# A conditioned transformer block on one core: two more products of the ff residual taken by a second level of seven products, seven big tiles in place of eight

## The chip, the cores and the metric

The kernel runs on one NeuronCore of one Trainium2 chip. The metric is the device time of one execution in microseconds (us), the median of several runs; a profile of one execution stands beside it. The engines are called as the profile calls them: PE is the matrix engine (PEld its weight loads), DVE the vector engine, ACT the scalar engine, POOL the GpSimd engine, SP the engine whose queue issues most DMAs. [...]

## The reference

The input x is 2 x 2048 rows of 512 floats, with a condition t of 512 floats for each half. All is float32.

```python
emb = silu(t) @ ada_w + ada_b
shift_msa, scale_msa, gate_msa, shift_mlp, scale_mlp, gate_mlp = split(emb, 6)
norm  = ln(x) * (1 + scale_msa) + shift_msa
h     = gelu_exact(norm @ ssm_w1 + ssm_b1)            # 512 -> 512
x     = x + gate_msa * (h @ ssm_w2 + ssm_b2)          # 512 -> 512: the ssm residual
norm2 = ln(x) * (1 + scale_mlp) + shift_mlp
hf    = gelu_tanh(norm2 @ ff_w1 + ff_b1)              # 512 -> 1024
x     = x + gate_mlp * (hf @ ff_w2 + ff_b2)           # 1024 -> 512: the ff residual
```

## The kernel before

**Tiles and blocks.** The 4096 rows are cut into eight blocks of 512 rows (128 partitions x 4 chunks). A block's x, its normalised and transposed form nT, hA (the ssm's hidden layer) and hClo and hChi (the two halves of the ff's hidden layer) are "big" tiles of 1 MB each, from a pool of eight. A tile asked for when all are in use takes over one whose last user comes earlier in program order, and waits for that user.

**Seven products for eight.** A matrix product is split into 2 x 2 quarters and computed from seven products P1 to P7 of quarters and of sums of quarters. The sums (`sums_of_first` for one operand, `sums_of_second` for the other) are made by POOL or DVE. A product accumulates in one of three PSUM banks, called y (P1, P6, P7, P4), x (P2) and v (P5, P3), and DVE adds the bank to the residual tile after each product, so that what a bank holds is always the sum that the next quarter of the result needs. In the residuals the banks are seeded with the bias row, by ACT.

**The ff residual.** For blocks 1 to 7 this is `residual_in_leaves`. P1, P5, P6 and P7 are "plain": eight fp32 matmuls with 256 columns (16 records in the trace, L724), read by DVE at L735. P2, P3 and P4 go by a second level: each is split into seven again. These are the leaves: two fp32 matmuls with 128 columns each (four records, L757). The loop over the leaves has seven turns, one for each of LEAVES = P1, P2, P6, P5, P7, P3, P4; in a turn PE does that leaf of P2 and of P3, which lie side by side in one bank and are read by one 256-wide add (L773), then that leaf of P4, in a bank of its own, read by a 128-wide add (L776). Two matmuls of plain P7 are put into each of the first four turns, and P7 is read in turn 4. Block 0 uses seven plain products (`residual`, L465 and L687).

**The order of the work.** It is written out by hand: each engine gets its instructions in program order, and work that is not the current stage's is hung on "hooks", places between products of the current stage. From block 1 on, one pass of the main loop (i = 1 to 7) does in PE's order:

1. the ff products of block i (`Second.products`, L881): 26 products by a longer scheme; its operand "forms" are 20 sums made from nT of the second norm (L819, on POOL, in the pass before), and its results are added by ACT (L895) and DVE (L898) and put through gelu by ACT (L876);
2. the ssm residual of block i+1 (oA, L465 and L687), which ends with the second norm's statistics of block i+1 (L499, L500);
3. the ff residual of block i (oC);
4. the ssm hidden layer of block i+2 (hA, L465).

In the last two passes some of these stages have no block left. A norm is: statistics on DVE, `scales` on POOL (L508 to L526), `normal` on ACT (L539), `turn` on DVE (a transpose inside 32 x 32 blocks, L550), `move` (16 DMAs of 64 KB, L559, on SP's queue or shared with ACT's), and `moved` on ACT (scale and shift, L582). The first norm of block i+2 is made during stage 1 of pass i, the second norm of block i+1 during stage 3.

In stage 3, the first product's hook holds the load of x of block i+3, the scales and normalisation of the second norm and the sums of nT of block i+2; after P5, after P6 and in the turns come the transposes, the move and the statistics of block i+3. The sums for the leaves of P2 and P4 ("sums24", four adds of 128 x 512) and of P3 ("sums3", four of 128 x 256) are made by POOL in stage 2. From block 4 on the gates of the second half of the batch apply: w2 and fw2 are loaded again and multiplied by the new gate on DVE (L395), which is set off in blocks 2 and 3.

Of the kernel before, what the change touches and what calls it, by code (L numbers as in the profile page):

```python
# [140 lines left out]
def kernel(  # L141
# [16 lines left out]
    nc = tc.nc  # L158
# [13 lines left out]
    big = ctx.enter_context(tc.tile_pool(name="big", bufs=8))  # L172
# [58 lines left out]
    brows = big_tile("brows")  # L231
# [176 lines left out]
    fw2_t = const.tile([P, 3, 3, KD // 2, P], F32, tag="fw2_t", name="fw2_t")  # L408
# [3 lines left out]
    single_t = fw2_t[:, 2]  # L412

    def leaves_of_weight(w_sb, s, eng):


        def views(w):
            v = w.rearrange("p (h k) (q e d) -> p h k q e d", h=2, e=2, d=P)
            return {f"{h + 1}{e + 1}": v[:, h, :, :, e, :] for h in range(2) for e in range(2)}

        hi = w_sb[:, w_sb.shape[1] // 2 :, :]
        q23, q4 = views(hi), {n: v[:, :, 0, :] for n, v in views(s[:, 2]).items()}
        t23, t4 = thirds(pair_t), thirds(single_t)
        o23, o4 = second_operands(q23, t23), second_operands(q4, t4)
        ops = {
            "P2": {n: v[:, :, 0, :] for n, v in o23.items()},
            "P3": {n: v[:, :, 1, :] for n, v in o23.items()},
            "P4": o4,
        }
        return ops, sums_of_second(q23, t23, eng) + sums_of_second(q4, t4, eng)  # L430
# [7 lines left out]
    def seed(name, row, part):  # L438


        b, cols = (("y", row[:, : D // 2]), ("v", row[:, D // 2 :]))[part]
        t = ps_g.tile([P, 2, HT], F32, tag=b, name=f"p{b}_{name}_{len(seeds.get((name, b), ()))}")
        seeds.setdefault((name, b), []).append(t)
        nc.scalar.copy(t, cols.unsqueeze(1).to_broadcast([P, 2, HT]))
# [41 lines left out]
    class Norm:  # L486
# [44 lines left out]
        def normal(self, c, eng=None, on_pe=False):  # L531

            if c == 0:
                self.nT = big_tile(f"nT{self.name}")
                self.xn = self.blocks().rearrange("p m k c q -> p m (k c q)") if on_pe else self.nT
# [172 lines left out]
    def residual_in_leaves(name, i, hops, wops, leaf_wops, kdim, hooks, last=False, read_p7=4):  # L708
# [3 lines left out]
        F = D // 2  # L712
        q = {
# [26 lines left out]
        for p, dests, n in (("P1", ("11",), "P1"), ("P5", ("22", "12"), "P2"), ("P6", ("12",), "P6")):  # L740
            run(plain(p))
            read(p, *dests)
            hooked(n)

        tags = {("P23", "y"): "t", ("P23", "x"): "x", ("P23", "v"): "x", ("P4", "y"): "t", ("P4", "x"): "y", ("P4", "v"): "v"}
        leaf_ps = {
# [3 lines left out]
        started = set()  # L750

        def leaf(which, n, f):
            t = leaf_ps[which, LEAF_BANK[f]]
            fresh = (which, LEAF_BANK[f]) not in started
            started.add((which, LEAF_BANK[f]))
            for k in range(KD // 2):
                nc.tensor.matmul(  # L757
                    t[:, n, :],
                    hops.leaves["P4" if which == "P4" else ("P2", "P3")[n]][f][:, k, :],
                    leaf_wops["P4" if which == "P4" else ("P2", "P3")[n]][f][:, k, :],  # L760
                    start=((fresh or f == "P2") and n == 0 and k == 0),
                    stop=(f in ("P2", "P3", "P4") and k == KD // 2 - 1),
                    skip_group_check=True,
                )

        p7 = list(plain("P7"))
        places = {1: "P5", 2: "R2", 3: "P7", 4: "R4", 5: "P3", 6: "P4"}
        for r, f in enumerate(LEAVES):
            t, e = LEAF_AT[f]
            for n in range(2):  # L770
                leaf("P23", n, f)
            d = xt[:, t, :].rearrange("p (q d) -> p q d", q=2)[:, :, e * P : (e + 1) * P]
            nc.vector.tensor_tensor(d, leaf_ps["P23", LEAF_BANK[f]][:, :2, :], d, ALU.add)  # L773
            leaf("P4", 0, f)
            d = xt[:, 2 + t, e * P : (e + 1) * P]
            nc.vector.tensor_tensor(d, leaf_ps["P4", LEAF_BANK[f]][:, 0, :], d, ALU.add)  # L776
            if r == read_p7:
                read("P7", "22", "21")
# [10 lines left out]
            now, p7 = p7[: PLAIN_P7[r]], p7[PLAIN_P7[r] :]  # L789
            run(now)  # L790
            if r in places:
                hooked(places[r])
# [48 lines left out]
    class Second:  # L841


        def __init__(self, i):
            self.i, self.lo, self.hi = i, big_tile(f"hClo_{i}"), big_tile(f"hChi_{i}")
            self.parts = {}
# [61 lines left out]
        def summed(self, g, eng, cut=1):  # L908
            s = thirds(sums.tile([P, 3, 2, HT], F32, tag="s", name=f"hSC_{self.i}_{g}"))
# [8 lines left out]
        def leaf_sums(self, room24, room3, eng):  # L918


            v = self.hi.rearrange("p (g k) (q e t) -> p g k q e t", g=2, q=2, e=2)
            q24 = {f"{e + 1}{g + 1}": v[:, g, :, :, e, :] for e in range(2) for g in range(2)}
            q3 = {
                f"{e + 1}{g + 1}": self.parts[g]["P3"][:, :, e * P : (e + 1) * P]
                for e in range(2)
                for g in range(2)
            }
            s24 = thirds(room24.rearrange("p (s k q t) -> p s k q t", s=3, k=2, q=2))
            s3 = thirds(room3.rearrange("p (s k t) -> p s k t", s=3, k=2))
            o24, o3 = first_operands(q24, s24), first_operands(q3, s3)  # L930
# [3 lines left out]
                "P3": o3,  # L934
            }
            return sums_of_first(q24, s24, eng), sums_of_first(q3, s3, eng)

        def leaf_room(self, nxt, nx2):
            L = 3 * KD // 2 * P
            if nxt and not nx2:  # L940
                return [big_tile(f"leaves_{self.i}_{n}").rearrange("p a b -> p (a b)")[:, : m * L] for n, m in ((0, 2), (1, 1))]
            flat = forms.rearrange("p n a r -> p (n a r)")
            return flat[:, : 2 * L], flat[:, 2 * L : 3 * L]
# [212 lines left out]
    fold, late_forms = None, []  # L1156


    for i in range(1, NBLK):
        nxt, nx2, last = i + 1 < NBLK, i + 2 < NBLK, i + 1 == NBLK  # L1160
# [4 lines left out]
        if i == 1:  # L1165
            leaf_wops, ops = leaves_of_weight(fw2_sb, fw2_s, nc.gpsimd)
            hook(hooks, (5, 7, 9, 11, 13, 14, 15, 16), ops)
        if i == 1:
            hook(hooks, (0,), [n1[i + 2].scales])
        if nxt:  # L1170
            hook(hooks, (1, 2, 3, 4), hA[i + 1].summed(nc.gpsimd))
        if nxt:
            hook(hooks, (20, 24), [lambda p=p: seed(f"oA_{i + 1}", gb[2], p) for p in range(2)])
        else:
            hook(hooks, (20, 24), [lambda p=p: seed(f"oC_{i}", gb[5], p) for p in range(2)])
        if nx2:
            hook(hooks, (12, 14, 16, 18), [lambda c=c: n1[i + 2].normal(c) for c in range(C)])
            hook(hooks, (14, 16, 18, 20), [lambda c=c: n1[i + 2].turn(c) for c in range(C)])
            hook(hooks, (20,), [n1[i + 2].move])
        if fold:  # L1180
            hook(hooks, (0,), fold[:2])
            hook(hooks, (5,), fold[2:6])
        hook(hooks, (0, 0, 0, 1), late_forms)
# [6 lines left out]
        late_forms = []  # L1190
# [3 lines left out]
        sums24, sums3 = hC.leaf_sums(*hC.leaf_room(nxt, nx2), nc.gpsimd)  # L1194
        hook(hooks, ("P5",), sums24)
        hook(hooks, ("P7",), sums3)
        if nxt:
# [3 lines left out]
            if fold:  # L1201
                hook(hooks, ("P1", "P2", "P6", "P5"), fold[6:10])
            hook(hooks, ("P2", "P6"), [lambda p=p: seed(f"oC_{i}", gb[5], p) for p in range(2)])
# [6 lines left out]
        leaf_fold, fold = fold and fold[10:], None  # L1210

        hooks = {}
        if i + 3 < NBLK:
            n1[i + 3] = Norm(i + 3, 1)
            hook(hooks, ("P1",), [lambda: load_x(i + 3)])
        if nxt:

            hook(hooks, ("P1",), [lambda: n2[i + 1].scales(on_dve=not nx2)])
            hook(hooks, ("P1",), [lambda c=c: n2[i + 1].normal(c) for c in range(C)])
# [5 lines left out]
        if i + 3 < NBLK:  # L1225
            hook(hooks, ("P5", "P7", "P3", "P4"), n1[i + 3].stats())
            hook(hooks, ("P4",), [n1[i + 3].scales])
# [10 lines left out]
        if not last:  # L1238
            hook(hooks, ("P4",), [lambda: store(i, 0)])
        refold5 = (i + 1) % PER_B == 0 and nxt  # L1240
        if refold5:
            b = (i + 1) // PER_B
            gb[5], multiply_5 = gate_bias(5, b, fb2, f"gb5_{b}")
            hook(hooks, ("P7",), [lambda: load_half("fw2", fw2, fw2_sb, 0)])
        if nxt:
# [7 lines left out]
            if not nx2:  # L1253

                def late_form(n):
                    if n == 0:
                        late["ops"] = form((nc.vector,) * 12 + (nc.gpsimd,) * 8)
                    late["ops"][n]()

                late_forms = [lambda n=n: late_form(n) for n in range(len(HK_B))]  # L1260
                hook(hooks, ("P7",) * 4 + ("R4",) * 4, late_forms[:8])
                late_forms = late_forms[8:]

        residual_in_leaves(f"oC_{i}", i, hC, fw2_ops, leaf_wops, KH // 2, hooks, last, 4 if nx2 or last else 6)
        if refold5:
            load_half("fw2", fw2, fw2_sb, 1)
        if not last:
# [4 lines left out]
        if refold5:  # L1272
            take_gate(5, b)
            fw2_ops, fold = weight_of_second(fw2_sb, fw2_s, gate[5, b], (nc.vector,))
            leaf_wops, ops = leaves_of_weight(fw2_sb, fw2_s, nc.vector)
            fold += ops
        hooks = {}
        if refold5:
            hook(hooks, ("P6",), [multiply_5])
            hook(hooks, ("P5", "P5", "P7", "P3", "P4", "P4"), fold[:6])  # L1280
            fold = fold[6:]
        if refold2:
            take_gate(2, b)
            w2_ops, w2_fold = weight_of_second(w2_sb, w2_s, gate[2, b], (nc.vector,))
            hook(hooks, ALL, [multiply_2] + w2_fold)
        if nx2:
            hA[i + 2] = First(i + 2, n1[i + 2].ops, hooks)
# [45 lines left out]
```

## Time and profile before

| | us |
|---|---|
| median of 3 runs | 594.19 (592.70 to 594.46) |
| profiled execution | 592.64 |
| its span, first to last instruction | 590.8 |
| outside the span | 1.8 |

| engine | busy us | share of the span |
|---|---|---|
| PE | 581.2 | 98% |
| PEld | 512.9 | 87% |
| DVE | 402.6 | 68% |
| POOL | 396.1 | 67% |
| ACT | 236.0 | 40% |

The granted clock of PE is 1.000 over the span. Busy time of PE is the union of records whose ends are modelled: a record overlaps the next one, so that PE can be 98% busy and its instructions still start at an even pace. The pace is read from the starts.

### The profile page before, as it was taken

What the parts mean: (1) busy time and instruction counts of PE and PEld (TensorE: products, weight loads), DVE (VectorE), ACT (ScalarE), POOL (GpSimd) and SP (SyncE); (2) the same over time, 40 slices, a digit from 0 to 9 for tenths busy, and PEclk for the clock granted to TensorE, in tenths of its full rate; (3) what the DMA queues carried; (4) which work ended last, traced back from release to release, by engine and by line L of the source; (5) the groups of instructions that cost most, each with busy time, mean ns of one, the idle gap of its engine ahead of it and who ended that gap; (6) DMA issues with size and microseconds to landing.
All of it is one profiled execution on the core that took longest, in us unless ns stands there. A gap on an engine that the chain in (4) does not pass through costs nothing.

```text
span 590.8 us, 8982 instructions
## 1 busy us (share of the span) xinstructions
PE 581.2 (98%) x3127; PEld 512.9 (87%) x3127; DVE 402.6 (68%) x723; ACT 236.0 (40%) x400; POOL 396.1 (67%) x480
## 2 busy tenths in 40 slices
PE   7999999999999999999999999999999999998997
PEld 4888888888889888998889988898888988897886
DVE  4978888897567475675755778874756446569663
ACT  2235457305532364234721456124553236222420
POOL 1875359999980968539984599948687294804260
PEclk9999999999999999999999999999999999999999
DMA  8990333300324104440152702231030400031002
GB/s 317 395 388 11 86 72 79 101 37 36 72 73 116 46 0 103 155 136 2 24 137 60 226 1 50 94 72 72 1 72 1 143 2 1 1 72 71 1 1 72
DMA packets 24376, 50.17 MB, mean 85 GB/s; under 512 B 4576, under 2 KB 5644, under 8 KB 23436
## 3 DMA queue, kind: packets, MB, share of 16 engines
q1 hardware_dynamic: 20608, 44.86, 24.5%
q10 hardware_dynamic: 3724, 4.75, 3.3%
q8 instruction: 25, 0.41, 0.3%
q14 instruction: 19, 0.16, 0.1%
HBM read 26.51 MB, written 8.40 MB: 59 GB/s over the span
## 4 chain that ended last, share of the span: by engine, by line
PE 95%; DVE 2%; DMA 2%; SPq 0%; issue 0%
PE py_oC L724 12%; PE px_hC L881 10%; PE py_hA L465 9%; PE py_oA L465 9%; PE py_hC L881 8%; PE pv_hC L881 8%; PE pl_oC_P_y L757 6%; PE pv_hA L465 5%; PE pv_oA L465 5%; PE pv_oC L724 4%; PE pl_oC_P_v L757 3%; PE px_hA L465 2%; PE py_oC L465 2%; PE py_hC L465 2%; PE px_oA L465 2%; DMA ada<-in_L_cond_ada_w_dram 2%
## 5 line engine op out<-in xcount | busy, mean ns | idle before, releaser
L582 ACT ACTIVATE nT<-nT,mod,mod 128x512 f32<-128x512 f32 x54 | 39.6, 803 | 103.0 <-DMA nT<-blocks 54.1
L539 ACT ACTIVATE nT<-x,nmr,rstd 128x512 f32<-128x512 f32 x56 | 42.5, 804 | 52.9 <-POOL nmr L526 38.0
L724 PE MATMUL py_oC<-fw,hClo 128*128 128x256 f32 x224 | 54.1, 379 | 0.0
L508 POOL TENSOR_SCALAR ve<-mv 128x4 f32<-128x4 f32 x16 | 3.7, 232 | 72.4 <-DVE mv L500 65.7
L499 DVE BATCH_NORM_STATS2 st<-x 128x6 f32<-128x512 f32 x64 | 43.4, 678 | 5.2 <-DMA x<-in_x_dram 4.9
L347 POOL TENSOR_TENSOR hSC<-hClo,hChi 128x512 f32<-128x512 f32 (+1 forms) x17 | 20.5, 1213 | 37.9 <-ACT hChi L876 24.4
L724 PEld LDWEIGHTS py_oC<-fw,hClo 128*128 128x128 f32 x224 | 40.4, 190 | 4.3
L881 PE MATMUL py_hC<-forms,fw 128*128 128x256 f32 x168 | 40.8, 379 | 0.0
L898 DVE TENSOR_TENSOR hClo<-hClo,py_hC 128x512 f32<-128x512 f32 x42 | 28.5, 681 | 17.3 <-ACT hClo L895 9.6
L819 POOL TENSOR_TENSOR forms<-forms 128x256 f32<-128x256 f32 x51 | 38.1, 748 | 3.0
L550 DVE STREAM_TRANSPOSE blocks<-nT 128x512 f32<-128x512 f32 x56 | 38.0, 695 | 1.6 <-ACT nT L539 1.2
L819 POOL TENSOR_TENSOR forms<-nT,forms 128x256 f32<-128x256 f32 x38 | 27.7, 749 | 15.9 <-DVE forms L819 15.4
L881 PEld LDWEIGHTS py_hC<-forms,fw 128*128 128x128 f32 x168 | 31.8, 190 | 4.4
L687 DVE TENSOR_TENSOR x<-py_oA,x 128x512 f32<-128x512 f32 x32 | 22.0, 688 | 19.4 <-PE py_oA L465 14.3
L898 DVE TENSOR_TENSOR hChi<-hChi,pv_hC 128x512 f32<-128x512 f32 x35 | 23.3, 683 | 14.3 <-PE pv_hC L881 14.3
L465 PE MATMUL py_hA<-nT,w 128*128 128x256 f32 x128 | 30.4, 380 | 0.0
L881 PE MATMUL px_hC<-forms,fw 128*128 128x256 f32 x112 | 27.8, 380 | 2.1 <-DVE forms L819 2.1
L876 ACT ACTIVATE hClo<-hClo,colsT 128x256 f32<-128x256 f32 x56 | 25.3, 500 | 4.9 <-DVE hClo L898 4.4
L895 ACT ACTIVATE hClo<-px_hC 128x512 f32<-128x512 f32 x21 | 12.5, 597 | 35.0 <-PE px_hC L881 30.1
L465 PE MATMUL py_oA<-w,hA 128*128 128x256 f32 x112 | 26.5, 379 | 0.0
L465 PEld LDWEIGHTS py_hA<-nT,w 128*128 128x128 f32 x128 | 23.7, 190 | 3.1 <-DVE hA L639 0.2
L876 ACT ACTIVATE hChi<-hChi,colsT 128x256 f32<-128x256 f32 x56 | 25.1, 496 | 1.9 <-DVE hChi L898 1.9
(291 smaller groups left out, 1584.0 us busy)
## 6 DMA issues: line engine op xcount, KB each, us to landing
nT<-blocks SPq DMA_DIRECT2D x168, 64.0 KB
x<-in_x_dram SPq DMA_DIRECT2D x7, 1024.0 KB
out_dram<-x SPq DMA_DIRECT2D x14, 512.0 KB
ada<-in_L_cond_ada_w_dram SPq DMA_DIRECT2D x6, 1024.0 KB
fw<-in_L_cond_ff_w_dram SPq DMA_DIRECT2D x2, 2048.0 KB
nT<-blocks ACTq DMA_DIRECT2D x56, 64.0 KB
w<-in_L_cond_ssm_w_dram SPq DMA_DIRECT2D x3, 1024.0 KB
fw<-in_L_cond_ff_w_dram SPq DMA_DIRECT2D x2, 1024.0 KB
```

The source lines that it names most:

```text
L465: nc.tensor.matmul(ps[b][j * apart][:, j, :], lhs(p, j, k), rhs(p, j, k), start=(fresh and j * (not apart) == 0 and k == 0), stop=(p in (" ...
L499: nc.vector.bn_stats(st, xs[self.i][:, c, :])
L539: nc.scalar.activation(t, x_c, AF.Identity, bias=self.nmr[:, c : c + 1], scale=self.rstd[:, c : c + 1])
L550: nc.vector.transpose(self.bl[:, :, :, c, :].rearrange("p m k q -> p k m q"), self.nT[:, c, :].rearrange("p (k m q) -> p k m q", k=KD, m=C),)
L582: nc.scalar.activation(dst, src, AF.Identity, bias=shift, scale=scale)
L687: nc.vector.tensor_tensor(d, ps[BANK[p]][:, js], d, ALU.add)
L724: yield lambda j=j, k=k: nc.tensor.matmul(ps[BANK[p]][:, j, :], hops(p, j, k), wops[p][:, k, :], start=False, stop=(k == kdim - 1), skip_g ...
L757: nc.tensor.matmul(t[:, n, :], hops.leaves["P4" if which == "P4" else ("P2", "P3")[n]][f][:, k, :], leaf_wops["P4" if which == "P4" else ( ...
L819: eng.tensor_tensor(reg[d], reg[a], reg[b], ALU.add if f == "+" else ALU.subtract)
L876: nc.scalar.activation(h, h, AF.Gelu_apprx_tanh, bias=fb1T[:, m : m + 1])
L881: nc.tensor.matmul(ps[b][:, j, :], fa[ra][:, j * P : (j + 1) * P], fb[rb].rearrange("p a (c q) -> p c a q", q=Q), start=(fresh and j == 0) ...
L898: nc.vector.tensor_tensor(dest(d), dest(d), ps[b], op)
```

## The change

In blocks 2, 3, 5, 6 and 7 (`five`) of the ff residual, P5 and P7 go by the second level too, so that five of the seven products are in leaves and only P1 and P6 are plain. A turn there is: the leaf of P2 and P3, its read; the leaf of P5, its read; the leaf of P4, its read; the leaf of P7, its read. The leaves of P7 lie in the rooms (banks) of P4's leaves, at the next 128 columns; those of P5 lie in the seeded v bank, and its x leaf in the x room of P4. P6 follows P1 directly, is read in turns 1 and 2 (once as one 1024-wide add for two quarters).

The operands of the new leaves are sums again: "sums35" is P3's and P5's together (128 x 512), "sums7" is P7's. For the weights they are made once for each gate, in a larger `fw2_t`, which also holds at the start what a big tile (`brows`) held. The pool of big tiles has seven. From block 2 on the first norm overwrites x (nT is the same tile), and x of block i+1 is loaded a second time at the start of pass i, for the residuals. The load of x of block i+3 moves from the first product's hook of stage 3 to turn 2, and the statistics of block i+3 move from stage 3 to stage 4 (hA of block i+2); their scales move to the next pass. P1, P6 and P5 of hA are read by ACT. In block 3 both halves of fw2 are loaded after the residual; before, one half was loaded within it. In block 6, the 20 forms of the last block are all hung on turn 4.

The diff, cut to its core:

```diff
-    big = ctx.enter_context(tc.tile_pool(name="big", bufs=8))
+    big = ctx.enter_context(tc.tile_pool(name="big", bufs=7))
...
-        return ops, sums_of_second(q23, t23, eng) + sums_of_second(q4, t4, eng)
+        sums = {"P23": sums_of_second(q23, t23, engs["P23"])}
+        for j, (p, w) in enumerate((("P4", s[:, 2]), ("P5", s[:, 0]), ("P7", lo[:, :, D // 2 :]))):
+            q, t = {n: v[:, :, 0, :] for n, v in views(w).items()}, thirds(fw2_t[:, 2 + j])
+            ops[p] = second_operands(q, t)
+            sums[p] = sums_of_second(q, t, engs[p])
+        return ops, sums
...
-                self.nT = big_tile(f"nT{self.name}")
+                in_place = self.which == 1 and self.i >= 2
+                self.nT = xs[self.i] if in_place else big_tile(f"nT{self.name}")
...
+        if five:
+            run(plain("P1"))
+            read("P1", "11")
+            hooked("P1")
+            run(plain("P6"))
+            hooked("P2")
+        else:
+            for p, dests, n in (("P1", ("11",), "P1"), ("P5", ("22", "12"), "P2"), ("P6", ("12",), "P6")):
...
+        seeded = ps["v"].rearrange("p j d -> p (j d)").rearrange("p (n d) -> p n d", d=P)
+        place = {("P2", b): (rooms["P23", b], 0) for b in "yxv"}
+        place |= {("P3", b): (rooms["P23", b], 1) for b in "yxv"}
+        place |= {("P4", b): (rooms["P4", b], 0) for b in "yxv"}
+        place |= {("P7", b): (rooms["P4", b], 1) for b in "yxv"}
+        place |= {("P5", "y"): (seeded, 0), ("P5", "v"): (seeded, 1), ("P5", "x"): (rooms["P4", "x"], 2)}
...
-        places = {1: "P5", 2: "R2", 3: "P7", 4: "R4", 5: "P3", 6: "P4"}
+        places = {1: ("P5",), 2: ("R2",), 3: ("P7",), 4: ("R4",), 5: ("P3",), 6: ("P4",)}
+        if five:
+            places = {0: ("P6",), 2: ("P5",), 3: ("R2",), 4: ("P7",), 5: ("R4", "P3"), 6: ("P4",)}
         for r, f in enumerate(LEAVES):
             t, e = LEAF_AT[f]
+            for p in ("P2", "P3"):
+                leaf(p, f)
+            add(X[:, 0, t, :, e, :], place["P2", LEAF_BANK[f]][0][:, :2, :])
+            if five:
+                add(X[:, :, t, 1, e, :], leaf("P5", f))
+            add(X[:, 1, t, 0, e, :], leaf("P4", f))
+            if five:
+                add(X[:, 1, t, :, e, :], leaf("P7", f))
+            if five and r == 1:
+                read("P6", "12")
+            if five and r == 2:
+                nc.vector.tensor_tensor(
+                    xt[:, 2:4, :].rearrange("p t (q d) -> p t q d", q=2),
+                    ps["y"].unsqueeze(2).to_broadcast([P, 2, 2, F]),
+                    xt[:, 2:4, :].rearrange("p t (q d) -> p t q d", q=2),
+                    ALU.add,
+                )
...
+        five = i % PER_B != (1 if i < PER_B else 0)
...
         if nxt:
+            hook(hooks, (0,), [lambda: load_x(i + 1)])
             hook(hooks, (1, 2, 3, 4), hA[i + 1].summed(nc.gpsimd))
+        if nx2 and i > 1:
+            hook(hooks, (5,), [n1[i + 2].scales])
...
-            hook(hooks, ("P1",), [lambda: load_x(i + 3)])
+            hook(hooks, ("P5",), [lambda: load_x(i + 3)])
+        if last:
+            hook(hooks, ("P1",), sums7)
+        elif nx2:                                   # and five
+            hook(hooks, ("P1",), sums35)
...
-        if i + 3 < NBLK:
-            hook(hooks, ("P5", "P7", "P3", "P4"), n1[i + 3].stats())
-            hook(hooks, ("P4",), [n1[i + 3].scales])
...
-                hook(hooks, ("P7",) * 4 + ("R4",) * 4, late_forms[:8])
-                late_forms = late_forms[8:]
+                hook(hooks, ("P7",), [lambda n=n: late_form(n) for n in range(len(HK_B))])
...
         if nx2:
-            hA[i + 2] = First(i + 2, n1[i + 2].ops, hooks)
+            hA[i + 2] = First(i + 2, n1[i + 2].ops, hooks, on_act=("P1", "P6", "P5"))
```

## The prediction

> **What bounds the kernel now.** I read the head of the page, then what the matrix engine waited for, then the timelines of the matrix engine (PE) and the vector engine (DVE) through the ff residual of block 3. The page:
>
> ```profile
> span 590.8 us, 8982 instructions
> PE 581.2 (98%) x3127; PEld 512.9 (87%) x3127; DVE 402.6 (68%) x723; ACT 236.0 (40%) x400; POOL 396.1 (67%) x480
> PE 95%; DVE 2%; DMA 2%; SPq 0%; issue 0%
> ```
>
> PE is busy for 98% of the span and carries 95% of the chain that ended last. So PE's own work counts in full, and so does every new wait of PE. Its waits of today, in the whole run:
>
> ```profile
> PE px_hC L881 <- DVE forms L819: 2.1, 1, 2.1
> PE pada L274 <- DMA ada<-in_L_cond_ada_w_dram: 1.7, 2, 1.5
> PE idle L970 <- POOL ident masks.py:199: 1.3, 1, 1.3
> ```
>
> None is in the residual that is changed. PE there (start, length, then the instruction):
>
> ```profile
> 305.44 3.62 PE L724 MATMUL py_oC<-fw,hClo 128*128 128x256 f32 x16
> 308.89 3.62 PE L724 MATMUL pv_oC<-fw_s,hSC 128*128 128x256 f32 x16
> ...
> 318.00 0.61 PE L757 MATMUL pl_oC_P_x<-fw,hChi 128*128 128x128 f32 x4
> 318.45 0.61 PE L757 MATMUL pl_oC_P_x<-fw,hSC 128*128 128x128 f32 x4
> 318.89 0.61 PE L757 MATMUL pl_oC_P_x<-fw_s,hChi 128*128 128x128 f32 x4
> 319.34 1.03 PE L724 MATMUL py_oC<-fw,hClo 128*128 128x256 f32 x4
> ```
>
> A plain product starts 3.45 us before the next; a leaf starts 0.447 us before the next ((319.34-318.00)/3). A leaf's results are there 0.61 us after its start, which is later than the start of the leaf behind it. The reads by DVE:
>
> ```profile
> 309.16 0.69 DVE L735 TENSOR_TENSOR x<-py_oC,x 128x512 f32<-128x512 f32 x1 [0.43 <-PE py_oC L724]
> ...
> 319.09 0.42 DVE L773 TENSOR_TENSOR x<-pl_oC_P_x,x 128x256 f32<-128x256 f32 x1 [0.69 <-PE pl_oC_P_x L757]
> 319.54 0.29 DVE L776 TENSOR_TENSOR x<-pl_oC_P_x,x 128x128 f32<-128x128 f32 x1
> ```
>
> The read of P4's leaf (L776) begins 0.04 us after that leaf's end and ends at 319.83. PE has long gone on to another bank, 0.49 us earlier. That overlap is what the kernel lives on.
>
> **The change, part by part.**
>
> *Removed and added on PE.* In five blocks (2, 3, 5, 6, 7) P5 and P7, plain until now, become seven leaves each: 2 x (3.45 - 7 x 0.447 = 0.32) = 0.65 us saved a block, 3.2 us in all. That is the whole possible gain on PE, 0.5%.
>
> *New waits of PE.* The order of the changed program, with the semaphores that each instruction waits for, shows what the diff only hints at. P7's leaf accumulates in the bank of P4's leaf (column 1 beside column 0 of the same room), directly behind it, and waits for DVE's read of P4's leaf in all seven turns. In turn 1, P5's leaf is in that room too, so P4's leaf waits for the read of P5's. And P6 plain, which had P5 plain (another bank) between itself and P1, now follows P1 in the same bank and waits for the read of P1. That is 9 waits a block, 45 in all, each for a read that cannot begin before the instruction just ahead on PE has ended. In the kernel before, the shortest such loop (P6 plain, its read, P7 plain) has three leaves of other banks, 1.3 us, in it. PE works in order, so everything behind the waiting leaf is held.
>
> *The price of a wait.* A read's end to PE's restart: the one PE wait on DVE in the trace ended so:
>
> ```profile
> 541.18 1.78 DVE L819 TENSOR_TENSOR forms<-forms 128x256 f32<-128x256 f32 x3
> 543.11 1.10 PE L881 MATMUL px_hC<-forms,fw 128*128 128x256 f32 x4 [2.10 <-DVE forms L819]
> ```
>
> That is 542.96 to 543.11, 0.15 us, and the group then takes 1.10 in place of 1.03 us: 0.22 us. At the start of the run a group of py_hA began 0.06 us after DVE's end and lost 0.10 more, 0.16 us. With these two ends:
> - P4 to P7: 319.83 + 0.16 to 0.22 against 319.34, so 0.65 to 0.72; I take 0.70, x 7 = 4.9 us.
> - P5 to P4 in turn 1: the read is the 0.42 form in place of 0.29: 0.83 us.
> - P1 to P6: the read ends at 309.85, plus 0.22, against 308.89: 1.2 us.
>
> Sum 6.9 us, less 0.65 saved: 6.3 us a block.
>
> *DVE's queue in front of these reads.* Before, two transposes of the norm (1.29 us a pair) stood ahead of turn 0; now the second pair stands between turns 0 and 1. Laying the reads out turn by turn (a turn is some 2.95 us long, its four reads take 1.2 us of DVE), the pair ends some 0.5 us after turn 1's first read is ready, and the new 1024-wide read of P6 (about the 1.28 us that the pair of 512-wide reads takes) puts turn 3's back by 0.4 us: 0.9 us in blocks 2, 3 and 5; 0.4 in 6 and 7, which turn earlier. Bounds: nothing, where DVE catches up within the turn, and 2 us, where both delays count in full.
>
> *Block 6* computes the last block's 20 forms in DVE's and POOL's queues at one place (turn 4) and no longer in part behind the residual. PE's wait of 2.1 us at 541 us should go, since POOL then has two turns and two products in front of the reader; four adds of 0.42 us on DVE ahead of turn 5 put about 0.6 us back. *Block 7* has no ssm residual as cover: before, DVE read P1 at 568.73, 2.1 us after its end at 566.66, because it was still adding up hSC. P6 now waits for that read: 3.1 us, 1.9 more than elsewhere.
>
> *What is hidden.* The second-level sums grow on POOL by four 128x256 shapes to 128x512 (0.75 to 1.28 us each) and four more of 0.75: about 5 us a block. POOL waits 65.7 us in 13 stretches for mv (L508) today, and P3/P5's sums fill that; if that cover were gone, the forms would be late by up to 5 us, but a residual longer by 7 us gives more time than that. DVE gets 14 reads of 0.42 and one of 1.28 for four of 0.69 (+4.4 us a block of 70), and three reads of hA a block go to ACT, 40% busy. The statistics of the next-but-two block leave the residual for hA, where DVE has gaps of 0.4 to 1.0 us between reads. The second load of x (1 MB, six times) stands on SP behind the store of the block two before, whose tile it takes, and ahead of the norm's 16 moves; it is wanted only 36 us after that store is issued (12 of hA, 22.6 of ff products, one product), and the 1 MB and the stores around 330 us had landed within 9 us: no cost. Normalising in place changes no wait on PE. In block 3 both halves of fw2 now load after the residual (the first 4.5 us later than before), and DVE's fold may hold hA's reads: 0 to 2 us once. I take 0, because DMA traffic had ended by 338 us, when that read is due.
>
> *Sum.* Blocks 2, 3, 5: 3 x 7.2 = 21.5; block 6: 6.3 + 0.4 + 0.6 - 2.1 = 5.2; block 7: 6.3 + 0.4 + 1.9 = 8.6. Together 35.3 us on the profiled execution's 592.64 (span 590.8): 627.9. That execution lies 1.55 us below the median of 594.19, at the lowest of the three runs, so I say 628.
>
> [...] The row: P4's and P7's leaves write disjoint columns, yet the order holds P7's leaf until DVE's L776 has read P4's. [...]
>
> [...]
>
> **The rivals.**
> - *The waits are free* (other side): if the reads were done when PE arrives, PE keeps 3.2 us and the 2.1 us of block 6: 592.64 - 5.3 = 587.3. It decides from a read that ends less than 0.45 us after P4's leaf starts. The trace has 0.94 us (318.89 to 319.83), so I give it 2%. No change at all would need the waits to cost a tenth of my price: 1%.
> - *The waits are cheaper*: if PE restarts with the read's end and DVE never queues, a leaf costs 0.49, the others 0.62 and 0.96, 5.0 - 0.65 = 4.4 a block, 22 us, less 2.1: 612. 12%.
> - *A transfer becomes the bound*: x's second load or fw2 late, by the 9 us that loads and stores took around 330 us, in two or more blocks, on top of the waits: 646 and above. It is against the slack of some 20 us. 5%.
> - The forecast, waits as priced: 80%.
>
> **How the numbers follow.** The range takes the cheap rival's upper half and, above, 2 us for fw2, 2 us of queueing in each block for 0.4 to 0.9, and the dearer restart: 616 to 638. A measurement of this kernel tells 0.3% (1.8 us) from no change; faster by more has 0.02, within it 0.01, slower 0.97.
>
> **What would show it right or wrong.** Right: PE's waits list P7's and P4's leaves behind DVE's leaf read, some 40 times with about 0.5 us of idle each (the leaf's tail counts as busy), and P6 plain behind the read of P1 five times at about 1 us; PE's busy share falls to some 94%; five residuals last 30 us in place of 23.2, those of blocks 1 and 4 stay; the wait at L881 goes. Wrong: a PE share that stays at 98%, waits on DMA or POOL in front of the ff products, or a granted clock below 1.

## The result: 51 us slower, and the profile after

The changed kernel takes 644.66 us (643.79 to 646.16), the kernel before 593.5 in the same series: a ratio of 1.086, interval 1.083 to 1.090. The profiled execution took 643.95 us, its span is 642.2, 51.4 more than before. I had forecast 35.3 more. The direction and the mechanism are there; 16 us are missing from the sum. The head of the page and its chain:

```profile
span 642.2 us, 9376 instructions
PE 593.3 (92%) x3247; PEld 519.1 (81%) x3247; DVE 433.5 (68%) x779; ACT 247.5 (39%) x430; POOL 424.3 (66%) x502
PE 66%; DVE 16%; POOL 7%; issue 4%; ACT 4%; DMA 2%; SPq 0%; DVEq 0%; ACTq 0%; POOLq 0%
```

PE has gone from 98% to 92% of the span, and DVE and POOL have entered the chain, 16% and 7%. What PE waited for (us in total, times, longest):

```profile
PE pl_oC_P_y L777 <- DVE x L791: 16.4, 20, 4.0
PE pl_oC_P_v L777 <- DVE x L791: 8.4, 10, 1.4
PE py_oC L732 <- DVE x L743: 7.3, 5, 2.9
PE pl_oC_P_x L777 <- DVE x L791: 6.7, 10, 1.2
...
PE px_hC L921 <- DVE hChi L938: 1.8, 2, 1.0
...
PE px_hC L921 <- ACT hClo L935: 0.4, 1, 0.4
```

The first four lines are the 45 waits of the prediction: 40 of a leaf behind a leaf's read (L791), 5 of P6 plain behind the read of P1 (L743). The last two are new and lie in the ff products of blocks 1 and 4. The wait for the forms (L881 before) is gone. PE in the residual of block 3:

```profile
315.58 3.62 PE L732 MATMUL py_oC<-fw,hClo 128*128 128x256 f32 x16
320.14 3.69 PE L732 MATMUL py_oC<-fw_s,hSC 128*128 128x256 f32 x16 [0.94 <-DVE x L743]
...
325.01 0.61 PE L777 MATMUL pl_oC_P_y<-fw_s,hChi 128*128 128x128 f32 x4
327.10 0.71 PE L777 MATMUL pl_oC_P_y<-fw,hClo 128*128 128x128 f32 x4 [1.48 <-DVE x L791]
...
330.38 0.71 PE L777 MATMUL pl_oC_P_x<-fw_s,hChi 128*128 128x128 f32 x4 [1.23 <-DVE x L791]
331.48 0.71 PE L777 MATMUL pl_oC_P_x<-fw,hClo 128*128 128x128 f32 x4 [0.38 <-DVE x L791]
```

P6 starts 1.11 us later than right behind P1 (320.14 - 315.58 - 3.45; priced at 1.2). The leaf of P7 in turn 1 (331.48) waits 0.38 us and takes 0.71 in place of 0.61: that is the priced loop. But in turn 0 it waits 1.48 us (327.10). DVE at that time shows why:

```profile
324.60 1.42 DVE L557 STREAM_TRANSPOSE blocks<-nT 128x512 f32<-128x512 f32 x2 [4.60 <-ACT nT L546]
325.94 0.39 DVE L791 TENSOR_TENSOR x<-pl_oC_P_y,x 128x256 f32<-128x256 f32 x1
326.43 0.42 DVE L791 TENSOR_TENSOR x<-pv_oC,x 128x256 f32<-128x256 f32 x1
326.77 0.28 DVE L791 TENSOR_TENSOR x<-pl_oC_P_y,x 128x128 f32<-128x128 f32 x1
...
328.19 1.30 DVE L557 STREAM_TRANSPOSE blocks<-nT 128x512 f32<-128x512 f32 x2
```

DVE stood idle for 4.60 us before the first pair of transposes, which waited for ACT's normalised chunks. The reads of turn 0 are queued behind that pair. ACT had waited for POOL. Here is where POOL begins the norm's scales, first before the change, then after it, where ACT's line stands last:

```profile
308.82 0.23 POOL L508 TENSOR_SCALAR ve<-mv 128x4 f32<-128x4 f32 x1 [1.31 <-DVE mv L500]
```

```profile
315.49 1.29 POOL L348 TENSOR_TENSOR forms<-hSC,hSC 128x512 f32<-128x512 f32 x1
...
319.31 1.27 POOL L348 TENSOR_TENSOR forms<-hSC,forms 128x512 f32<-128x512 f32 x1
320.66 0.23 POOL L514 TENSOR_SCALAR ve<-mv 128x4 f32<-128x4 f32 x1
...
323.75 2.93 ACT L546 ACTIVATE nT<-x,nmr,rstd 128x512 f32<-128x512 f32 x4 [5.94 <-POOL nmr L532]
```

Before, POOL stood waiting for the statistics and began 3.38 us after the residual's first matmul (308.82 - 305.44). Now the four adds of sums35 stand ahead, and it begins 5.08 us after (320.66 - 315.58).

Cut into stages, each from its first matmul to the first of the next stage, the two timelines of PE give (us):

| | before | after | more | forecast |
|---|---|---|---|---|
| residuals of blocks 2, 3, 5 | 23.19 each | 31.86, 31.91, 31.57 | 25.8 | 21.5 |
| residual of block 6 and the ff products behind it | 23.19 + 24.79 | 37.08 + 22.45 | 11.6 | 5.2 |
| residual of block 7 | 23.36 | 34.01 | 10.7 | 8.6 |
| ff products of block 1 | 22.46 | 23.90 | 1.4 | 0 |
| ff products of block 4 | 22.49 | 24.37 | 1.9 | 0 |

The residuals of blocks 1 and 4 stay (23.2), and everything else moves by 0.1 us in all. In block 6 the long wait and what follows it, first DVE, then POOL at the same time, then PE, then PE's windows (start and end, length, PE busy, PEld, DVE, ACT, POOL, granted clock, DMA share and GB/s):

```profile
550.35 1.23 DVE L522 TENSOR_TENSOR e<-r,ve 128x4 f32<-128x4 f32 x1 [0.88 <-POOL r L516]
551.61 0.16 DVE L523 SCALAR_TENSOR_TENSOR e<-e,r 128x4 f32<-128x4 f32 x1
551.81 1.12 DVE L524 SCALAR_TENSOR_TENSOR rstd<-e,r 128x4 f32<-128x4 f32 x1
552.96 1.20 DVE L525 SCALAR_TENSOR_TENSOR nmr<-mv,rstd 128x4 f32<-128x4 f32 x1
555.17 2.83 DVE L557 STREAM_TRANSPOSE blocks<-nT 128x512 f32<-128x512 f32 x4 [1.02 <-ACT nT L546]
```

```profile
550.29 1.27 POOL L348 TENSOR_TENSOR leaves<-hSC,hSC 128x512 f32<-128x512 f32 x1
551.64 1.27 POOL L348 TENSOR_TENSOR leaves<-leaves,hSC 128x512 f32<-128x512 f32 x1
552.87 1.26 POOL L348 TENSOR_TENSOR hSC<-hSC 128x512 f32<-128x512 f32 x1
```

```profile
559.09 1.22 PE L777 MATMUL pl_oC_P_y<-fw,hClo 128*128 128x128 f32 x4 [3.99 <-DVE x L791]
```

```profile
559.00:561.00 2.00, 1.91 (x9) 1.92 (x10) 0.46 (x2) 0.00 (x0) 0.00 (x0) 0.53 0.82 186
561.00:563.00 2.00, 1.76 (x9) 1.57 (x8) 0.62 (x2) 0.00 (x0) 0.00 (x0) 0.62 0.87 206
```

Three of the four scale operations on 128 x 4 elements take 1.1 to 1.2 us. Each of them ends within 0.03 us of the POOL add beside it (551.58 and 551.56, 552.93 and 552.91, 554.16 and 554.13); the fourth, which falls where one add ends and the next begins, takes 0.16. PE waits 3.99 us for the reads behind the transposes, and then its clock is half for some 3.4 us (0.53 and 0.62 in these windows, which reach beyond it): leaf groups take 1.22 and 1.06 us in place of 0.71 and 0.61. In block 7, P6 waits 2.88 us and then takes 5.28 us in place of 3.69.

### The profile page after: what moved, and what is told of

It is laid out like the page before. It is cut to its first block, busy times and chain, and to the rows that moved or that the text cites. A ratio compares the mean times of both kernels' runs of the same rounds, so it can differ in the third digit from the quotient of the medians.

```text
span 642.2 us, 9376 instructions
## 1 busy us (share of the span) xinstructions
PE 593.3 (92%) x3247; PEld 519.1 (81%) x3247; DVE 433.5 (68%) x779; ACT 247.5 (39%) x430; POOL 424.3 (66%) x502
## 4 chain that ended last, share of the span: by engine, by line
PE 66%; DVE 16%; POOL 7%; issue 4%; ACT 4%; DMA 2%; SPq 0%; DVEq 0%; ACTq 0%; POOLq 0%
PE py_hA L471 8%; PE px_hC L921 8%; DVE x L791 7%; PE py_hC L921 6%; PE pl_oC_P_y L777 6%; PE pv_hC L921 6%; PE py_oA L471 5%; PE py_oC L732 5%; PE pv_hA L471 4%; POOL forms L348 3%; PE pl_oC_P_v L777 2%; PE pv_oA L471 2%; PE py_hC L471 2%; PE px_hA L471 2%; PE pl_oC_P_x L777 2%
## 5 line engine op out<-in xcount | busy, mean ns | idle before, releaser
L791 DVE TENSOR_TENSOR x<-pl_oC_P_y,x 128x256 f32<-128x256 f32 (+1 forms) x76 | 28.0, 370 | 29.2 <-PE pl_oC_P_y L777 28.5
L589 ACT ACTIVATE nT<-nT,mod,mod 128x512 f32<-128x512 f32 x30 | 22.0, 803 | 64.5 <-DMA nT<-blocks 48.4
L546 ACT ACTIVATE nT<-x,nmr,rstd 128x512 f32<-128x512 f32 x32 | 23.4, 803 | 51.5 <-POOL nmr L532 32.2
L859 POOL TENSOR_TENSOR forms<-nT 128x256 f32<-128x256 f32 x12 | 9.1, 757 | 44.3 <-DMA x<-in_x_dram 28.4
L732 PE MATMUL py_oC<-fw_s,hSC 128*128 128x256 f32 x112 | 27.3, 399 | 7.3 <-DVE x L743 7.3
L732 PE MATMUL py_oC<-fw,hClo 128*128 128x256 f32 x144 | 33.5, 379 | 0.0
L589 ACT ACTIVATE x<-x,mod,mod 128x512 f32<-128x512 f32 x24 | 17.6, 802 | 39.3 <-DMA x<-blocks 39.3
L732 PEld LDWEIGHTS py_oC<-fw_s,hSC 128*128 128x128 f32 x112 | 22.0, 200 | 12.2 <-issue 4.6
L557 DVE STREAM_TRANSPOSE blocks<-nT 128x512 f32<-128x512 f32 x32 | 21.4, 695 | 14.4 <-ACT nT L546 14.4
L732 PEld LDWEIGHTS py_oC<-fw,hClo 128*128 128x128 f32 x144 | 26.7, 190 | 3.3
L938 DVE TENSOR_TENSOR hChi<-hChi,pv_hC 128x512 f32<-128x512 f32 x35 | 23.2, 680 | 8.8 <-PE pv_hC L921 8.8
```

The costliest lines, as they stand in the source:

```text
L546: nc.scalar.activation(t, x_c, AF.Identity, bias=self.nmr[:, c : c + 1], scale=self.rstd[:, c : c + 1])
L589: nc.scalar.activation(dst, src, AF.Identity, bias=shift, scale=scale)
L732: yield lambda j=j, k=k: nc.tensor.matmul(ps[BANK[p]][:, j, :], hops(p, j, k), wops[p][:, k, :], start=False, stop=(k == kdim - 1), skip_g ...
L791: nc.vector.tensor_tensor(d, src, d, ALU.add)
L859: eng.tensor_tensor(reg[d], reg[a], reg[b], ALU.add if f == "+" else ALU.subtract)
L938: nc.vector.tensor_tensor(dest(d), dest(d), ps[b], op)
```

## The experiments

**Reads after the turn's last leaf.** In each turn the five leaves run first; the reads of P5, P4 and P7 come after P7's leaf.

```diff
-                add(X[:, :, t, 1, e, :], leaf("P5", f))
-            add(X[:, 1, t, 0, e, :], leaf("P4", f))
-            if five:
-                add(X[:, 1, t, :, e, :], leaf("P7", f))
+                at = [(X[:, :, t, 1, e, :], leaf("P5", f)), (X[:, 1, t, 0, e, :], leaf("P4", f)), (X[:, 1, t, :, e, :], leaf("P7", f))]
+                for d, src in at:
+                    add(d, src)
+            else:
+                add(X[:, 1, t, 0, e, :], leaf("P4", f))
```

> In the five changed blocks each turn runs all its five leaves first (P2, P3, P5, P4, P7) and only then reads P5's, P4's and P7's. By the program's semaphores no leaf of P4 or P7 then waits for a read of the same turn; a room is written again only one or two turns later. Theory (the loss is the 40 waits of a leaf for the read of the leaf just ahead of it in its bank): the waits at L777 behind the reads, 31.5 us in the profile of the changed kernel, and some 0.1 us of slower restart each go, P6's five waits (7.3 us) stay: 606 to 612 us, PE busy share back to about 97%. Rival (DVE, with 4.4 us more reads a block, has no room and the reads only come late elsewhere): PE then waits at the next turn's leaves instead, and the time stays above 625 us.

Measured: 607.3 us (one run), span 605.5, PE 96%. The theory holds: 37 us go, with nothing taken out of PE or DVE, only the order changed. What PE still waits for in the residuals:

```profile
PE py_oC L732 <- DVE x L743: 7.3, 5, 2.9
PE pv_oC L777 <- DVE x L791: 4.3, 10, 0.9
...
PE pl_oC_P_y L777 <- DVE x L791: 0.7, 1, 0.7
```

The residuals of blocks 2, 3 and 5 last 25.0 us, those of 6 and 7 28.05 and 26.34. P6's five waits are unchanged at 7.3 us in all. A remainder of 5.0 us in 11 waits is of leaves waiting for the reads of the turn before.

**Turn 0 between P1 and P6.**

```diff
             run(plain("P1"))
             read("P1", "11")
-            hooked("P1")
-            run(plain("P6"))
-            hooked("P2")
...
+            if five and r == 0:
+                hooked("P1")
+                run(plain("P6"))
+                hooked("P2")
```

> Only turn 0's five leaves and their reads are put between P1 and P6 plain (and ahead of the hooks of P1 and P6); the reads inside a turn stay as in the changed kernel. Theory: P6's five waits for the read of P1 (7.3 us, and the half clock behind the one of block 7) go, and turn 0's reads stand ahead of the transposes in DVE's queue, so the 1.44 us wait of turn 0 in blocks 2, 3 and 5 falls to about 0.4 and the 3.99 us of block 6 too: 7.3 + 0.5 + 1.6 + 3 x 1 + 3.4 + 1.5 (half clock of block 6) = 17 us less, 626 to 631 us. Rival (the delay passes on to turn 1, whose reads now stand behind the same transposes): 634 to 640 us.

Measured: 637.63 us (one run); the rival is right. P6's waits are gone, but the transposes now stand in front of turn 1's reads, and the leaf of P4 there waits 1.38 to 1.43 us in blocks 2, 3 and 5 and 3.98 us in block 6. As long as a leaf of every turn waits for the read before it, moving the transposes behind turn 0 only moves the delay to turn 1. Blocks 2 and 5 (31.13 and 31.16 us) differ from block 3 (29.81) by a stretch at half clock behind that wait (granted clock 0.55 and 0.50 over 3 us), which block 3 does not have (1.00): 1.3 us.

**Both.**

> Both of the above. By the semaphores, none of the 45 waits is left. Theory (the change costs nothing but these waits and the queue in front of the reads): PE keeps the 3.2 us of shorter products and the 2.1 us of block 6, less the 2.8 us that blocks 1 and 4 lost in the ff products: 590 to 594 us, the kernel before at 593.5. Rival (DVE's longer reads or POOL's longer sums bind once the waits are gone): 600 us and above, with PE waiting on DVE or POOL at the leaves.

Measured: 601.48 us, ratio 1.0125 (1.0095 to 1.0155). Of the 45 waits only P6's in block 7 still holds PE, for 0.6 us, yet the rival's bound is met. The remaining waits of PE at the leaves are of another kind:

```profile
PE pv_oC L774 <- DVE x L788: 5.2, 10, 2.1
```

They are leaves of P5 in the seeded bank. Its y and v leaves share that bank, so that a leaf, mostly in turns 3 and 4, waits for the read of the turn before, when DVE is still late from the transposes and P6's reads. Residuals: 23.7 to 24.0 us in blocks 2, 3, 5, 27.1 in block 6, 24.7 in block 7. The products of blocks 1 and 4 are still 23.8 and 24.4.

**The rest of the change alone.** `five` is False everywhere, and the sums for P5's and P7's leaves are left out.

> P5 and P7 plain in all blocks as before; everything else of the change stays (seven big tiles, x loaded twice and normalised in place, moved statistics and forms, reads of hA on ACT); the leaf sums for P5 and P7 are left out. Theory: the rest of the change is worth about nothing: the 2.1 us wait of block 6 goes, the products of blocks 1 and 4 are 0.9 and 1.9 us longer: 592 to 596 us. Rival (a good part of the 16 us that the forecast missed comes from the rest, the second load of x or the moved statistics): 600 to 608 us.

Measured: 594.58 us, ratio 1.0007 (0.9991 to 1.0023). The theory holds, but "worth nothing" is a sum: the products of block 1 (+1.3) and block 4 (+1.9) lose most of what the products behind block 6's residual, those of block 7, gain (24.79 to 22.45). So the two losses are there without the new leaves too.

**The scales first.** The changed kernel, with POOL's order altered:

```diff
-        elif nx2:
-            hook(hooks, ("P1",), sums35)
...
             hook(hooks, ("P1",), [lambda: n2[i + 1].scales(on_dve=not nx2)])
+            if five and not nx2:
+                hook(hooks, ("P1",), [lambda: nc.gpsimd.tensor_copy(unread, n2[i + 1].nmr)])
             if five:
-                hook(hooks, ("P1",), sums7 if nx2 else sums35)
+                hook(hooks, ("P1",), sums35 + sums7 if nx2 else sums35)
```

> The changed kernel with one thing moved on POOL: in blocks 2, 3 and 5 the norm's scales come ahead of the second-level sums of P3/P5 (sums35) and not behind them; in block 6 one small POOL copy that reads the scales' result stands ahead of sums35, so that POOL's adds can't run beside DVE's four small scale operations. Theory (the stall of turn 0 is the transposes in DVE's queue, and they are late through POOL's sums in blocks 2, 3, 5 and through DVE's scales, slowed beside POOL's 128x512 adds, in block 6): turn 0's wait falls from 1.1 to 1.5 us to about 0.5 in blocks 2, 3, 5 (about 1 us less each); in block 6 the last two scale operations take 0.16 to 0.4 us in place of 1.1 to 1.2, turn 0's wait falls from 3.99 to about 2 us and the half clock behind it (some 2 us) mostly goes: 637 to 641 us. Rival (the transposes are late for another reason): waits as before, 643 to 646 us.

Measured: 637.95 us (one run). Residuals of blocks 2 and 3: 30.80 and 30.83, each 1.1 us less, and turn 0's wait there is the 0.38 us of the priced loop; of block 6: 32.52, 4.6 less, turn 0's wait 0.95 us and no half clock behind it. DVE in block 6:

```profile
549.17 0.16 DVE L524 SCALAR_TENSOR_TENSOR rstd<-e,r 128x4 f32<-128x4 f32 x1
549.37 0.16 DVE L525 SCALAR_TENSOR_TENSOR nmr<-mv,rstd 128x4 f32<-128x4 f32 x1
```

The same instructions take 0.16 us when POOL is held, and 1.1 to 1.2 us beside its 128x512 adds. In block 5 the gain was eaten (31.57 to 32.23) by a half clock behind a wait of 1.22 us, one that the changed kernel has too (1.23), without a half clock.

**Gaps of chosen length.** In the version "both":

```diff
+    GAPS = {(2, 3): 3, (2, 5): 4, (3, 3): 5, (3, 5): 6, (5, 3): 7, (5, 5): 8, (7, 5): 9}
...
+                for _ in range(GAPS.get((i, r), 0)):
+                    nc.vector.tensor_tensor(xt[:, 0, :], xt[:, 0, :], xt[:, 0, :], ALU.max)
```

> The version with reads late and turn 0 first, with 3 to 9 needless DVE operations (128x512 maximum of x with itself, some 0.65 us each) ahead of P5's read in turns 3 and 5 of blocks 2, 3 and 5 and turn 5 of block 7, so that PE stands still once each for about 1, 1.6, 2.2, 2.9, 3.5, 4.2 and 4.9 us. Theory (the half clock follows an idle time above a length of about 3 us): granted clock 1.00 behind the first three, 0.5 behind the last three or four, some 1.7 us lost each; 622 to 632 us. [...]

Measured: 641.1 us (one run); the gaps came out longer than planned, 2.13, 2.52, 3.58, 4.50, 5.04, 7.05 and 5.34 us. Behind the first two the granted clock is 1.00, behind the other five it is 0.50 to 0.59. But the wait of block 6, which this version has from the one before, tells against length alone. The first row is behind the wait of 2.10 us of "both", the second behind the same wait (2.09 us) here:

```profile
538.30:541.70 3.40, 3.40 (x19) 3.40 (x18) 2.85 (x8) 0.95 (x2) 0.00 (x0) 0.52 0.48 107
```

```profile
570.14:573.00 2.86, 2.58 (x21) 2.39 (x21) 2.69 (x6) 0.00 (x0) 0.00 (x0) 1.00 0.88 206
```

In "both" the half clock begins 1.4 us after PE has restarted, here not at all. Likewise P6's wait in block 7 halves the clock in the changed kernel (2.88 us), not with the late reads (2.89 us, P6 takes 3.69). So from 3.6 us the half clock was there each time, and from 1.2 to 2.9 us it came behind some waits and not behind others. The seven gaps alone fall in order of length, as the theory has it; the waits of the other versions show that length alone does not decide. What decides in the middle was not settled.

**More waits taken away.** Besides both edits: P6's reads in turns 4 and 5, the scales ahead of the last of sums35, in block 6 sums7 and the scales on POOL, in block 4 the statistics behind the first seven products.

```diff
-            if five and r == 1:
+            if five and r == (1 if last else 4):
                 read("P6", "12")
-            if five and r == 2:
+            if five and r == (2 if last else 5):
...
-            hook(hooks, (2, 4), unread_stats)
+            hook(hooks, (7, 9, 10, 11), unread_stats)
...
-        engs = (nc.gpsimd, nc.gpsimd, nc.gpsimd if nx2 else nc.vector)
+        engs = (nc.gpsimd, nc.gpsimd, nc.gpsimd if nxt else nc.vector)
...
-            hook(hooks, ("P1",), sums35)
+            hook(hooks, ("P1",), sums35[:3] + [lambda: n2[i + 1].scales()] + sums35[3:] + sums7)
```

> Reads late and turn 0 first, and besides: P6's reads in turns 4 and 5 (last block as before), the scales ahead of the last of sums35 on POOL, in block 6 the scales on POOL ahead of sums35 and the sums of P7's leaves (sums7) on POOL, and in block 4 the norm's statistics behind the first seven ff products. Theory (everything that the change loses is waits for DVE, each of which is taken away here but block 1's): residuals of 22.6 to 22.9 us in blocks 2, 3, 5, 6, 24.5 in block 7, the products of block 4 22.5 and of block 1 23.8: 588 to 591 us, 0.5 to 1% faster than the kernel before. Rival (DVE or POOL is at its limit and the delays come back elsewhere): 595 us and above.

Measured: 593.24 us, ratio 0.9999 (0.9987 to 1.0011). The residuals of blocks 2, 3 and 5 now last 22.54, 22.54 and 22.53 us, which is 0.65 under the 23.19 of before: the gain on PE is real and exactly as counted. Block 4's products are at 23.0, so the moved statistics were 1.4 of its 1.9 us. Blocks 6 (24.32) and 7 (24.73) lose 1.1 and 1.4 us, in block 6 mostly by one wait of 1.21 us for DVE, and block 1's products are still at 23.8. Neither theory nor rival is right: not every wait was taken away, and the gains and these losses cancel.

**Three blocks.** P5 and P7 in leaves in blocks 2, 3 and 5 alone, and x_2's second load asked for later, which gives block 1's hClo another tile. (This version leaves out two operations: plain P5 and P7 of blocks 6 and 7 read two weight quarters that still hold a difference made for the leaves, so that only its time counts. The version after it puts them back.)

```diff
-        five = i % PER_B != (1 if i < PER_B else 0)
+        five = i in (2, 3, 5)
...
-            hook(hooks, (0,), [lambda: load_x(i + 1)])
+            hook(hooks, (7 if i == 1 else 0,), [lambda: load_x(i + 1)])
...
+        elif i == 5:
+            hook(hooks, ("P5",), [lambda: apart_leaves(gb[5], nc.gpsimd, ALU.add)])
```

> The version before this one with P5 and P7 by the second level in blocks 2, 3 and 5 alone (blocks 6 and 7 plain as in the kernel before), and the second load of x_2 put behind the first seven ff products of block 1, by which the tile pool gives block 1's hClo a tile that is free and no longer that of x_0, whose store was still under way. Theory (in blocks 6 and 7 DVE is too full for the finer reads, and block 1's 1.3 us are the wait of ACT for that store, the price of seven big tiles): residuals 22.5 us in blocks 2, 3, 5 and 23.2 to 23.4 in 6 and 7, products of block 1 22.5 and of block 4 23.0: span 587 us, time 588 to 590 us, 0.5 to 0.9% faster than the kernel before. Rival (block 1's products are late through DVE or the stores, not the tile): 23.8 there, time 590 to 591.5 us.

Measured: 589.99 us, ratio 0.9945 (0.9929 to 0.9961). Block 1's products are back at 22.45. ACT's wait in them, in the changed kernel and then here:

```profile
ACT hClo L935 <- DMA out_dram<-x: 2.3, 1, 2.3
```

```profile
ACT hClo L937 <- PE px_hC L923: 3.1, 2, 2.8
```

With seven tiles hClo took x_0's, whose store was still running; here it takes another and waits for PE alone.

**Three blocks, whole.** Two more DVE operations restore the weights:

```diff
+            undo = [later[2], later[6]]
...
+        if i == 6:
+            hook(hooks, (6, 8), undo)
```

> As the three-block version, with two more DVE operations (128x256) in the ff products of block 6: they put back the two quarters of the weights that the second level had replaced by differences, which the plain P5 and P7 of blocks 6 and 7 read. (The three-block version left these two out, and only its time counts.) Theory: two operations of 0.42 to 0.7 us in gaps of DVE cost nothing: 588.5 to 590.5 us, 0.4 to 0.7% faster than the kernel before. Rival (they push the products' reads of block 6): products of block 6 above 23 us, 591 us and more.

Measured: 589.22 us (589.11 to 589.43) against 592.91, ratio 0.9929 (0.9915 to 0.9944): 0.7% faster than the kernel before, and all of its computation is there. PE waits for nothing behind the start of the run (its waits there are 2.1, 1.3 and 0.2 us):

```profile
span 587.5 us, 9211 instructions
PE 578.6 (98%) x3199; PEld 514.0 (87%) x3199; DVE 414.9 (71%) x751; ACT 247.9 (42%) x430; POOL 419.2 (71%) x503
```

The sum from the stages: 3 x 0.65 of leaves and 2.34 in block 7's products, less 0.5 in block 4's, is 3.8 us; the span is 3.3 shorter. The larger part of this gain is the wait for the forms, which was gone in the rest of the change alone too; the leaves give the smaller part. A version with neither the leaves nor the two losses of blocks 1 and 4 was not run.

## Why the prediction was wrong by 16 us

The 16 us are four terms of the sum: DVE's queue in front of the reads (4.3), block 6 (6.4), block 7 (2.1) and the tiles and statistics, put at no cost (3.3). The half clock, put at no cost too, stands within the second and the third.

**Right.** The bound (PE), the 45 waits, one by one, and the price of a leaf's wait: steady turns of block 2 last 2.95 us (262.55 to 265.50), as laid out. The saving of 0.65 us a block was seen bare, at 22.54. P6's wait was 1.1 for 1.2 us. The 2.1 us at L881 went. The waits stay the largest part: reads late gave back 37 us, and both edits 43.

**"DVE's queue in front of these reads": 0.9 us a block, measured some 2.3** (25.8 us over three blocks, less 3 x 6.3 for the waits). My layout gave turn 0 no delay, because before the change the first pair of transposes was done when its reads came. It is not now: POOL runs four sums35 adds (some 5 us) ahead of the scales, so the normalised chunks and the transposes come later. I had counted POOL's longer sums as hidden behind its own waits for mv and asked only whether the forms would be late; the reader that mattered was DVE's queue, through scales, ACT and transposes. The scales first took 1.1 us each from blocks 2 and 3. This step missed 4.3 us over three blocks, 1.4 in each. The 0.3 beside turn 0's 1.1 lies in turns 1 to 3, behind the second pair of transposes and P6's reads; no run took it apart.

**"Block 6": 5.2 us, measured 11.6.** I priced the forms and not the norm. 4.6 us of the 6.4 missed come from the four scale operations beside POOL's adds and what follows from them: turn 0's wait (3.0) and the half clock (the rest, 1.5). Of the remainder, P6's wait is 0.6 longer than in other blocks: in DVE's timeline the four adds of sums7 stand ahead of the statistics, and these ahead of P1's read. The rest was not taken apart. Each scale operation took 0.16 us with POOL held (the scales first); in the changed kernel three of the four took 1.1 to 1.2 us beside POOL's adds of 1.27 us, and ended within 0.03 us of the add. That one holds up the other is my reading of these times; by what means was not shown. I had taken DVE's durations from rows in which POOL was not in the way.

**"Block 7": 8.6 us, measured 10.7.** P6 started 3.05 us later than right behind P1 (610.49 - 603.99 - 3.45), priced at 3.1. The half clock made the group 1.6 us longer (5.28 against 3.69), which is most of the 2.1 missed.

**The half clock, dismissed on one row.** In the kernel before I read a granted clock of 1.00 around its one wait of 2.1 us (541.0 to 543.1 us, and 1.00 still from 543.1 to 545.0) and took that for all waits, though I had named a granted clock below 1 as a sign of being wrong. The changed kernel makes longer ones (3.99 and 2.88) and pays some 3.1 us for them. Behind the chosen gaps it was 1.00 up to 2.52 us and 0.50 to 0.59 from 3.58 us on. The half clocks behind waits of 1.2 to 2.9 us, present in one version and absent in the next, show that no single pause of 3.58 us is needed.

**"No cost" for the second load of x, and gaps for the statistics: measured 3.3 us.** I followed the second load of x and found slack, but not the other tenant of the pool: with seven tiles hClo of block 1 takes the tile that x_0's store is still reading (1.4 us; shown by the three-block version). The statistics of block 4 I looked for in hA's gaps; two of the four stand in the ff products, between hChi's reads, beside the gate's fold:

```profile
363.43 0.68 DVE L396 TENSOR_TENSOR fw<-fw,pgate 128x512 f32<-128x512 f32 x1
364.03 0.68 DVE L505 BATCH_NORM_STATS2 st<-x 128x6 f32<-128x512 f32 x1
...
364.85 0.66 DVE L938 TENSOR_TENSOR hChi<-hChi,px_hC 128x512 f32<-128x512 f32 x1
```

The other 0.5 us there is left when the statistics are moved; the fold, one operation of which comes later than before, is the likely reason, not a shown one.

**The rivals.** "Waits are free" and "cheaper" are out. "A transfer becomes the bound" was right in kind for 1.4 us (the store under hClo), not in size. Whether P7's leaf could write its columns while DVE reads P4's was not tried; no run here shows it.

## What to carry to other kernels

When PE has to wait for a read of its own last result, the read's whole queue becomes part of PE's path (here one leaf waited 3.99 us where the loop alone took 0.38): price not only the loop but everything that any engine may put in front of it, through every step back to the statistics. Here no work had to go: the reads issued behind the turn's last leaf, and independent products between a product and its successor in the same bank, gave back 43 of 51 us. And look for the new tenant of each buffer when a pool shrinks, not only for the transfers that the change names.

## What the hardware did that I had not expected

- A DVE operation on 128 x 4 elements took 0.16 us alone and 1.1 to 1.2 us beside a 128x512 add of POOL, within 0.03 us of whose end it ended. In the same block DVE's 128x256 adds (sums7) took 0.9 to 1.5 us beside such adds and 0.41 when POOL was idle; POOL's adds took 1.26 to 1.46 us.
- PE's granted clock fell to about 0.5 behind each of the chosen gaps of 3.58 to 7.05 us and behind the changed kernel's wait of 3.99 us, and behind some, not all, waits of 1.2 to 2.9 us, in places only 1 to 1.8 us after PE had restarted. It stayed there for 3.4 us (block 6) and 3.2 us (block 7) in the changed kernel, and for 3.4 us in "both"; behind the gap of 3.58 us it lasted until 5.3 us after the restart. Three that could be priced cost 1.3, 1.5 and 1.6 us, so that a wait here can cost more than its length.
